# Moving vector work between the units of a fused attention and feed-forward kernel

## The chip, the cores and the metric

The kernel runs on one core of a Trainium2 chip. The metric is the device time of one execution in microseconds (us). Five engines work side by side, each through its own list of instructions in order: TensorE (PE; its weight loads are shown as PEld), VectorE (DVE), ScalarE (ACT), GpSimd (POOL) and SyncE (SP), which only sends transfers. They wait for each other by semaphores.

## What is computed

The input x has 8 sequences of 256 tokens with 256 features. The reference, cut to its core:

```
x = x + attention(layernorm(x), ctx, ctx, mask)   # causal, masked, softmax
y = layernorm(x)
h = silu(y @ w1.T * s1) * (y @ w2.T * s2)         # 256 -> 1024
h = gelu(h @ h1.T * s3)                           # 1024 -> 1024
h = gelu(h @ h2.T * s4)                           # 1024 -> 1024
x = x + h @ w3.T * s5                             # 1024 -> 256
```

All weights are -1, 0 or 1; the scales s1 to s5 are float32.

## The kernel before

**Blocks.** The 2048 tokens are cut into four blocks t = 0 to 3 of 512 tokens, and `pair(s)` (L822) takes two blocks through the feed-forward part: t0 = 2s and t1 = 2s + 1. Everything is held turned, features on the 128 partitions and 512 tokens along a row. One matmul is 128 x 128 weights by 128 x 512 values into one PSUM bank.

**Two parts per value.** TensorE reads a rounded float32 form. Every operand is therefore split: ACT makes the rounded part (oh, `parted`, L786; hyt in `casts`), and DVE the rest (ol, `rest`, L312; lyt in `rests`, L601). Each product runs once with either part.

**Seven products for eight.** The two 1024 x 1024 layers (n = 2 and 3) work on the two blocks together in a scheme of seven products of half size instead of eight. `a`, `b` are the upper and lower halves of block t0's hidden values, `c`, `d` those of t1, each in two pieces `[0]`, `[1]` of 128 x 1024. The scheme needs differences, made by DVE in `sub` (L846): T1 = c - a and T2 = d - T1 among them. Product 6 reads T2, product 5 reads T1.

**Units.** `pair` is a generator; what lies between two `yield` is a unit, 80 in each pair:

| units | work of TensorE |
|---|---|
| 0 to 7 | the gated layer of t0: for each o a product pa (w1), then pb (w2); ACT makes gate = silu(pa), DVE multiplies it with pb (L689) |
| 8 to 15 | layer 2, products 1 and 2 |
| 16 to 23 | the gated layer of t1 (c from units 16 to 19, d from 20 to 23) |
| 24 to 43 | layer 2, products 6, 5, 3, 7, 4, four units each |
| 44 to 63 | layer 3, products 1, 6, 5, 3, 7 |
| 64 to 67 | layer 3, product 2 (`second`, L934; tile p); DVE adds each bank to na (L942, recorded at L844) |
| 68 to 71 | layer 3, product 4 |
| 72 to 75 | last layer of t1 (tile po), `finish` (L696) makes res and stores it |
| 76 to 79 | last layer of t0, in the same way |

Before a product, `before_` (L914) fetches the weights after the next (POOL's queue, tile a) and makes the next operand.

**The plan.** After each unit, the loop at L1183 runs what `at` has put into `plan` for (s, unit), in the order in which it was put there (L1164 to L1182). Three kinds of work go in this way:

- The attention of a later block (`stages`, L454), a generator of which each entry runs one stage. Block 2 is prepared in the first pair, block 3 from unit 55 of the first pair to unit 13 of the second. Late stages: bn_stats and bn_aggr of the sum (`sums`, L257; stf and mvf), the root on ACT (sdf, L638), its reciprocal on DVE (L640), `on_all` (L386), which turns the statistics by TensorE (tmf), copies them by DVE (hmf) and spreads them over all partitions by SP's transfers through memory (mf), then `turned_x` (xst), the difference on DVE and the product on POOL (yf, L648 and L649), the casts (hyt), the rests (lyt) and the store of xst (kept).
- Quarter sums of the weights (`sum_up`, L769).
- Looks (`look_through`, L222): the weights are checked for values for which the two-part scheme would not be exact. A step sends the next piece of weights on SP (tile raw, 512 KB, three buffers) and, from the third step on, examines the piece sent two steps before: pieces of w1, w2 and w3 by a TENSOR_REDUCE on DVE (L212), pieces of h1 and h2 by a Sign on ACT (L216) and, a step later, a count on DVE (L218). Four steps are in the first pair, 21 in the second. At the end the verdict decides whether the whole is done again in plain float32.

**Banks.** PSUM has three pools of two buffers: `ps_mm` (p, po, pb of a pair's first block and pa of its second), `ps_x` (px_u, px_y, pa of the first block, and the first po of t0) and `ps_at` (attention, pb of the second block). A product into a bank waits until the reader of its last content is done: the na for p, L689 for pb, L700 for po, the gate for pa.

Of the kernel before, what the change touches and what calls it, by code (L numbers as in the profile page):

```python
# [74 lines left out]
def _network(ctx, tc, g, exact, flag):  # L75
# [20 lines left out]
    def new(p, shape, tag, name, dt=F32, **kw):  # L96
        return p.tile(shape, dt, tag=tag, name=f"{v}{name}", **kw)

    def groups(t):

        return ((0,), (1,)) if t == 0 else ((0, 1),)
# [54 lines left out]
    def keep_warm(times):  # L156
        if exact:
            return
        warm = ps_mm.tile([P, TB], F32, tag="mm", name="warm")
        for _ in range(times):  # L160
            nc.tensor.matmul(warm, lhsT=zeros[:, :P], rhs=zeros[:, :TB], start=True, stop=True)
# [116 lines left out]
    def normed(src, js, mv, y, name):  # L278
        scaled(src, range(NT)[tiles(js)], mv, turned_over(js, root(js, mv, name), name), y)
# [12 lines left out]
    def turned(y, js, name, pool_=None, tag="at", room=None):  # L292

        wide = len(js) * S
        room = room or TB // wide
        pieces = []
        for c0 in range(0, ND, room):
            pt = (pool_ or ps_at).tile([P, room, wide], F32, tag=tag, name=f"{v}{name}_{c0}")
            for c in range(room):
                for n, i in enumerate(range(NT)[tiles(js)]):  # L300
                    nc.tensor.transpose(  # L301
                        pt[:, c, bass.ts(n, P)], y[:, i, bass.ts(c0 + c, P)], ident
                    )
            pieces.append((slice(c0, c0 + room), pt))
        return pieces
# [6 lines left out]
    def rest(lo, value, hi):  # L312
        nc.vector.tensor_tensor(lo, value, hi.bitcast(F32), ALU.subtract)  # L313
# [22 lines left out]
    def table(t, js, func):  # L336

        if t == 0 and js == groups(t)[0 if func == AF.Exp else -1]:
            nc.scalar.activation(junk, eps, func)

    def near(t):

        return exact or t < 2
# [110 lines left out]
    def stages(t, js, once, result, xs, kt, vs, mi):  # L454
# [99 lines left out]
        if first_:  # L554
# [17 lines left out]
            def shifted(i, engine):  # L572
                engine.tensor_scalar(
                    y[:, i, :],
                    xs[:, i, :],
                    centre[:, i : i + 1],
                    std[:, i : i + 1],
                    ALU.add,
                    ALU.mult,
                )  # L580
# [20 lines left out]
        def rests(values):  # L601
            for c, value in values if not exact else ():
                rest(yt[1][:, c, cols], value, yt[0][:, c, cols])

        def turned_x():
            pxt = turned(xs, js, f"pxt_{t}_{js[0]}")
            if t:
                residual_turned(pxt)
            return pxt

        def residual_turned(pxt):
            for c, pt in pxt:
                nc.scalar.copy(xst[:, c, cols], pt)

        if near(t):
            y = once("y", "yf", [P, NT, D])
            if first_:
                residual_turned(turned_x())
                shifted(1, nc.vector)
            else:  # L620
                normed(xs, js, mvf, y, f"f_{t}_{js[0]}")
            table(t, js, AF.Silu)
            yield
            pxt = None if first_ else turned_x()
            if not t and js == groups(t)[-1]:
                keep_warm(WARM_LATER)
            yield

            where = () if t else (ps_mm, "mm") if first_ else (ps_x, "x", 1)
            values = turned(y, js, f"pyt_{t}_{js[0]}", *where)  # L630
            casts(values)
            if not t and not first_:
                residual_turned(pxt)
            yield
            rests(values)
        else:
            std = once("sq", "sdf", [P, NT], tiny, bufs=2)
            nc.scalar.activation(std, mvf[:, 1, :], AF.Sqrt, bias=eps)  # L638
            yield
            nc.vector.reciprocal(mvf[:, 1, :], std)  # L640
            yield
            mean, rstd = on_all(mvf, ("row", "row2"), f"mf_{t}")
            yield
            turned_x()
            yield
            y = once("y", "yf", [P, ND, TB])
            for c in range(ND):
                nc.vector.tensor_tensor(y[:, c, :], xst[:, c, :], mean, ALU.subtract)  # L648
                nc.gpsimd.tensor_tensor(y[:, c, :], y[:, c, :], rstd, ALU.mult)  # L649
            yield  # L650
            values = [(slice(c, c + 1), y[:, c : c + 1, :]) for c in range(ND)]
            casts(values)
            yield
            rests(values)
        if js == groups(t)[-1]:
            nc.sync.dma_start(out=kept(t), in_=xst)
        result[:] = yt
# [124 lines left out]
    def half(tag, name):  # L782

        return new(hp, [P, 2, TB], tag, name, bufs=2)
# [37 lines left out]
    def pair(s, places, stock):  # L822
# [9 lines left out]
        def two(names):  # L832
            return [[None, None] for _ in names]
# [12 lines left out]
        def sub(out, one, other):  # L846
            nc.vector.tensor_tensor(out, one, other, ALU.subtract)

        a, b, c, d, T1, T2 = two("abcdef")
# [13 lines left out]
        place = dict(zip(("a", "b", "c", "d", "T1", "T2", "free"), places))  # L863
# [33 lines left out]
        for n in (2, 3):  # L897
            first_, name = n == 2, f"{s}_{n}"
# [63 lines left out]
            if first_:  # L962
                for u in range(QK):
                    second(u)
                    yield
                X.pop(2)
                for o in range(NH):
                    mine, key, k = (c, "c", o) if o < QK else (d, "d", o - QK)
                    if k % 2 == 0:
                        mine[k // 2] = half(place[key], f"h{key}_{s}_{k}")  # L970
                    gated(
                        t1,
                        ready[t1],
                        o,
                        mine[k // 2][:, k % 2, :],
                        ps_mm.tile([P, TB], F32, tag="mm", name=f"pa_{t1}_{o}"),
                        ps_at.tile([P, TB], F32, tag="at", name=f"pb_{t1}_{o}"),
                    )
                    if not s and o in (2, 4):
                        fetch(o // 2 + 1)  # L980
                    if o in (2, 4):
                        T1[o // 2 - 1] = half(place["T1"], f"T1_{name}_{o}")
                        sub(T1[o // 2 - 1], c[o // 2 - 1], a[o // 2 - 1])

                    if o == 5:
                        T2[:] = [half(place["T2"], f"T2_{name}_{h}") for h in range(2)]
                        sub(T2[0], d[0], T1[0])
                    if o == 6:
                        X[6] = parted(T2[:1], f"{name}_6")
                        rest(X[6][0][1], T2[0], X[6][0][0])  # L990
                        sub(T2[1][:, 0, :], d[1][:, 0, :], T1[1][:, 0, :])
                    if o == 7:
                        hi, lo = (
                            new(hp, [P, 2, TB], f"op{i}", f"o{i}_{name}_6_1", FR, bufs=4)
                            for i in "hl"
                        )
                        X[6].append((hi, lo))
                        nc.scalar.copy(hi[:, 0, :], T2[1][:, 0, :])
                        sub(T2[1][:, 1, :], d[1][:, 1, :], T1[1][:, 1, :])
                        nc.scalar.copy(hi[:, 1, :], T2[1][:, 1, :])  # L1000
                        for k in range(2):
                            rest(lo[:, k, :], T2[1][:, k, :], hi[:, k, :])
                    yield
# [28 lines left out]
            for u in range(QK):  # L1032
                before_(3, u)
                product(stock[n, 3], X[3], x[u // 2][:, u % 2, :], u, start=False)
                if u % 2:
                    h = u // 2
# [9 lines left out]
            for u in range(QK):  # L1046
# [4 lines left out]
                if u % 2:  # L1051
                    h = u // 2
# [12 lines left out]
            for u in range(QK):  # L1065
# [4 lines left out]
                if u % 2:  # L1070
                    h = u // 2
# [7 lines left out]
            a, b, c, d, T1, T2 = na, nb, nc_, nd, nT1, nT2  # L1079
            place = at_  # L1080
# [53 lines left out]
    looking = look_through()  # L1134
# [6 lines left out]
    def at(s, units, action):  # L1141
        for unit in units if isinstance(units, (tuple, list, range)) else (units,):
            plan.setdefault((s, unit), []).append(action)
# [13 lines left out]
    def sums_from(r):  # L1157
# [5 lines left out]

    stages_at(1, (0, 0), (0, (1, 2, 4, 5, 7, 9, 10, 10, 10, 11, 13, 14)))  # L1164
    stages_at(
        2, (0, 8), (0, (25, 28, 30, 41, 45, 46, 49, 51, 53, 54, 55, 57, 58, 61, 62, 63))
    )
    stages_at(
        3, (0, 30), (0, (55, 56, 59, 70, 73, 74, 75, 77, 78, 79)), (1, (0, 1, 5, 8, 10, 13))
    )  # L1170
    at(0, (7, 7, 14, 15), lambda: next(summing[2], None))
    at(0, 9, lambda: sums_from(0))
# [1 line left out]
    at(0, 21, lambda: sums_from(1))  # L1174
    at(0, (32, 33, 34, 37), lambda: next(summing[4], None))
    at(0, 44, lambda: w3.extend(load_weight(g.w3t, "w3_")))
    at(0, (72, 74, 76, 78), lambda: next(looking, None))
    looks = (1, 3, 5, 8, 10, 12, 14, 16, 17, 19, 26, 27, 42, 44, 46, 47, 50, 51, 54, 55, 58)
    at(1, looks, lambda: next(looking, None))
    at(1, 61, lambda: [None for _ in looking])  # L1180
# [66 lines left out]
```

## Time and profile before

| what | value |
|---|---|
| median of three runs | 347.38 us (347.16 to 348.01) |
| the profiled execution's own time | 347.29 us |
| its span, first to last instruction | 345.4 us |
| busy: PE, DVE, ACT, POOL | 333.6, 270.1, 216.5, 36.5 us |
| chain that ended last | PE 87%, DVE 7%, ACT 2%, all else 4% |
| DMA | 68.81 MB, mean 199 GB/s |
| start of the first pair's units 17 and 24 | 61.04 and 73.87 us |
| start of units 64, 68, 72 of the first pair | 154.23, 162.24, 169.49 us |
| start of the second pair | 189.94 us |

A row of a timeline gives the start in us, the length in us, the engine, the line of the kernel, the operation, the tiles as out<-in, the shape and how many operations are merged; in brackets the idle time before it and what ended it. The view of waits gives who waited for whom, the total in us, how often and the longest.

### The profile page before, as it was taken

The page shows a single profiled execution, that of the slowest core. Times are in us where ns is not written, and L with a number is a line of the kernel's source. Part 1 is how long each engine was busy: PE and PEld are TensorE (multiplying, and loading weights), DVE is VectorE, ACT ScalarE, POOL GpSimd, SP SyncE. Part 2 cuts the span into 40 slices and gives each one's busy share as a digit, 9 for nine tenths or more (in the row PEclk, how much of TensorE's full clock was granted, in tenths as well). Part 3 has the DMA queues.
Part 4 walks back from the last instruction along what each step waited for, and adds up shares of the span by engine and source line. Part 5 has one row for each costly group of instructions (what it writes and reads, how often), then busy time and mean ns, then how long its engine had stood idle before and what let it go on. Part 6 is the DMA issues. An engine that isn't in the chain of part 4 may idle for free.

```text
span 345.4 us, 4324 instructions
## 1 busy us (share of the span) xinstructions
PE 333.6 (97%) x1505; PEld 269.6 (78%) x1506; DVE 270.1 (78%) x411; ACT 216.5 (63%) x300; POOL 36.5 (11%) x78
## 2 busy tenths in 40 slices
PE   8799999999999999999999999999999999999992
PEld 3677888787888888887888788887788888888781
DVE  5679866999799938687887894899957989756761
ACT  4668735358946755757672565556896688767630
POOL 3520000210001410022000003000001000000000
PEclk9999999999999999999999999999999999999998
DMA  5999981899396833369516482970644589630032
GB/s 184 344 297 272 254 297 61 319 316 278 133 361 238 244 123 121 131 240 328 188 74 232 143 258 99 283 283 28 227 139 138 164 260 372 225 121 0 0 122 71
DMA packets 20702, 68.81 MB, mean 199 GB/s; under 512 B 2465, under 2 KB 5313, under 8 KB 17090
## 3 DMA queue, kind: packets, MB, share of 16 engines
q0 software_dynamic: 7488, 36.70, 33.2%
q1 hardware_dynamic: 13040, 31.63, 26.8%
q8 instruction: 14, 0.23, 0.3%
q14 instruction: 14, 0.11, 0.1%
q10 hardware_dynamic: 146, 0.13, 0.1%
HBM read 55.86 MB, written 8.40 MB: 186 GB/s over the span
## 4 chain that ended last, share of the span: by engine, by line
PE 87%; DVE 7%; ACT 2%; issue 1%; DMA 1%; POOL 1%; POOLq 0%; ACTq 0%; DVEq 0%
PE px_u L813 34%; PE px_y L813 15%; PE po L1101 8%; PE p L813 7%; PE pa L673 7%; PE pb L673 6%; PE pv L528 3%; PE ps L467 3%; DVE ol L313 1%; PE pqt L301 1%; DVE sta L261 1%; PE pp L510 1%; PE pxt L301 1%; DMA xs<-x 1%; PE pa L879 1%
## 5 line engine op out<-in xcount | busy, mean ns | idle before, releaser
L813 PE MATMUL px_u<-oh,a 128*128 128x512 f32 x256 | 71.4, 394 | 0.4 <-ACT oh L796 0.4
L813 PE MATMUL px_u<-ol,a 128*128 128x512 f32 x256 | 70.8, 391 | 0.0
L813 PEld LDWEIGHTS px_u<-ol,a 128*128 128x128 f32 x256 | 47.9, 188 | 11.5 <-DVE ol L313 1.5
L813 PEld LDWEIGHTS px_u<-oh,a 128*128 128x128 f32 x256 | 47.6, 188 | 10.7 <-ACT oh L796 0.8
L686 ACT ACTIVATE gate<-pa,sc 128x512 f32<-128x512 f32 x32 | 21.8, 687 | 25.1 <-PE pa L673 22.5
L813 PE MATMUL px_y<-oh,a 128*128 128x512 f32 x128 | 34.5, 391 | 0.0
L813 PE MATMUL px_y<-ol,a 128*128 128x512 f32 x128 | 34.2, 389 | 0.0
L813 PEld LDWEIGHTS px_y<-ol,a 128*128 128x128 f32 x128 | 24.0, 188 | 5.0
L813 PEld LDWEIGHTS px_y<-oh,a 128*128 128x128 f32 x128 | 23.9, 188 | 5.0
L757 POOL DMA_DIRECT2D a<-S x16 | 8.5, 534 | 131.8 <-PE px_u L813 55.0
L216 ACT ACTIVATE sign<-raw 128x1024 bf16<-128x1024 f32 x16 | 16.9, 1055 | 7.0 <-DMA raw<-h2q 2.7
L218 DVE SCALAR_TENSOR_TENSOR sign<-raw,sign 128x1024 bf16<-128x1024 f32 x16 | 19.2, 1218 | 0.5 <-ACT sign L216 0.5
L673 PE MATMUL pa<-hyt,w 128*128 128x512 f32 x60 | 19.1, 399 | 0.2 <-DVE na L844 0.2
L673 PE MATMUL pb<-hyt,w 128*128 128x512 f32 x60 | 18.6, 391 | 0.2 <-DVE res L700 0.2
L673 PE MATMUL pa<-lyt,w 128*128 128x512 f32 x60 | 18.5, 390 | 0.0
L673 PE MATMUL pb<-lyt,w 128*128 128x512 f32 x60 | 18.5, 389 | 0.0
L841 ACT ACTIVATE nd<-nd,sc 128x512 f32<-128x512 f32 x16 | 10.7, 715 | 11.7 <-DVE nd L844 11.7
L813 PE MATMUL p<-oh,a 128*128 128x512 f32 x64 | 17.5, 394 | 0.4 <-DVE na L844 0.4
L313 DVE TENSOR_TENSOR ol<-nT,oh 128x1024 fp32r<-128x1024 f32 x12 | 14.5, 1221 | 3.9 <-ACT oh L796 3.8
L813 PE MATMUL p<-ol,a 128*128 128x512 f32 x64 | 17.1, 389 | 0.0
L844 DVE TENSOR_TENSOR na<-p,na 128x512 f32<-128x512 f32 x16 | 10.9, 688 | 7.9 <-PE p L813 7.9
L841 ACT ACTIVATE nb<-nb,sc 128x512 f32<-128x512 f32 x16 | 10.7, 717 | 10.1 <-DVE nb L844 7.4
(196 smaller groups left out, 649.7 us busy)
## 6 DMA issues: line engine op xcount, KB each, us to landing
a<-S POOLq DMA_DIRECT2D x16, 1024.0 KB, 5.0
a<-h1q POOLq DMA_DIRECT2D x6, 1024.0 KB, 8.1
a<-h2q POOLq DMA_DIRECT2D x6, 1024.0 KB, 5.1
raw<-h1q SPq DMA_DIRECT2D x8, 512.0 KB, 4.2
raw<-h2q SPq DMA_DIRECT2D x8, 512.0 KB, 5.1
vs<-ctx_n SPq DMA_DIRECT2D x4, 512.0 KB, 7.7
q<-h1q POOLq DMA_DIRECT2D x4, 512.0 KB, 20.4
q<-h2q POOLq DMA_DIRECT2D x8, 256.0 KB, 13.9
```

The source lines that it names most:

```text
L216: nc.scalar.activation(sign, raw, AF.Sign)
L218: nc.vector.scalar_tensor_tensor(sign, raw, 1.0, sign, ALU.mult, ALU.not_equal, accum_out=count[:, n : n + 1])
L313: nc.vector.tensor_tensor(lo, value, hi.bitcast(F32), ALU.subtract)
L467: nc.tensor.matmul(ps[:, a:e], lhsT=qt[:, c, bass.ts(2 * j + h, P)], rhs=kt[:, j, c, : e - a], start=(c == 0 and t > 0), stop=(c == ND - 1 ...
L528: nc.tensor.matmul(pv[:, h, :], lhsT=prt[:, j, bass.ds(a + k * P, P)], rhs=vs[:, 2 * j + k, :], start=(k == 0), stop=(k == n - 1),)
L673: nc.tensor.matmul(pm, lhsT=wc[:, bass.ts(o, P)], rhs=x, start=(n == 0), stop=(n == len(steps) - 1),)
L686: nc.scalar.activation(gate, pa, AF.Silu, scale=sc[:, 0, o : o + 1])
L757: nc.gpsimd.dma_start(out=a, in_=src)
L813: nc.tensor.matmul(bank, lhsT=a[:, k, bass.ts(o, P)], rhs=x[k // 2][part][:, k % 2, :], start=start and (part, k) == steps[0], stop=stop a ...
L841: nc.scalar.activation(out, src, AF.Gelu, scale=sc[:, n, o : o + 1])
L844: nc.vector.tensor_tensor(out, one, other, ALU.add)
L1101: nc.tensor.matmul(po, lhsT=w3[j * QK + k][:, bass.ts(o, P)], rhs=xs_[j][k // 2][part][:, k % 2, :], start=(j == 0 and (part, k) == STEPS[0]),
```

## The change

Four things move; no operation is added or taken away (the rests of blocks 2 and 3 stand apart instead of together).

- T1: both halves were made on DVE after the gated products of units 18 and 20. Now the first is made at unit 18, and the second at unit 21, behind the first half of T2.
- The rests: `rests` now yields after each of its two rests. Blocks 0 and 1 still run both at once. Block 2's were both at unit 63 of the first pair and are now at units 68 and 69, and the stage behind them (the store of xst, the handing over of the result) at unit 70. Block 3's were both at unit 13 of the second pair and are at 13 and 14.
- Block 3's `on_all` of the sum's statistics moves from unit 1 to unit 2 of the second pair.
- The four look steps of the first pair move from units 72, 74, 76, 78 to 70, 72, 74, 76.

```diff
         def rests(values):
             for c, value in values if not exact else ():
                 rest(yt[1][:, c, cols], value, yt[0][:, c, cols])
+                yield
...
-            rests(values)
+            list(rests(values))
...
-            rests(values)
+            yield from rests(values)
...
-                    if o in (2, 4):
-                        T1[o // 2 - 1] = half(place["T1"], f"T1_{name}_{o}")
-                        sub(T1[o // 2 - 1], c[o // 2 - 1], a[o // 2 - 1])
-
+
+
+                    if o == 2:
+                        T1[:] = [half(place["T1"], f"T1_{name}_{h}") for h in range(2)]
+                        sub(T1[0], c[0], a[0])
                     if o == 5:
                         T2[:] = [half(place["T2"], f"T2_{name}_{h}") for h in range(2)]
                         sub(T2[0], d[0], T1[0])
+                        sub(T1[1], c[1], a[1])
...
-        2, (0, 8), (0, (25, 28, 30, 41, 45, 46, 49, 51, 53, 54, 55, 57, 58, 61, 62, 63))
+        2, (0, 8), (0, (25, 28, 30, 41, 45, 46, 49, 51, 53, 54, 55, 57, 58, 61, 62, 68, 69, 70))
...
-        3, (0, 30), (0, (55, 56, 59, 70, 73, 74, 75, 77, 78, 79)), (1, (0, 1, 5, 8, 10, 13))
+        3, (0, 30), (0, (55, 56, 59, 70, 73, 74, 75, 77, 78, 79)), (1, (0, 2, 5, 8, 10, 13, 14, 14))
...
-    at(0, (72, 74, 76, 78), lambda: next(looking, None))
+    at(0, (70, 72, 74, 76), lambda: next(looking, None))
```

On the engines' lists this is: on TensorE tmf moves from behind pb of unit 1 to behind pb of unit 2; on DVE the second T1, the two lyt of block 2, one lyt of block 3, two reduces and the copy of tmf (hmf) move; on SP the four raw loads move ahead of the transfers of res and out beside them, and one of w3's ahead of mf; ACT and POOL keep their order.

## The prediction

> **What bounds the kernel now.** The page comes first: it names the full engine and shows whether its clock was held back.
>
> ```profile
> PE 333.6 (97%) x1505; PEld 269.6 (78%) x1506; DVE 270.1 (78%) x411; ACT 216.5 (63%) x300; POOL 36.5 (11%) x78
> PEclk9999999999999999999999999999999999999998
> ```
>
> TensorE is busy for 97% of the span, at full clock (digit 9) in all 40 slices but the last. The change removes none of its work, so it can win only where TensorE stands still. The view of waits, cut to 150 to 250 us and to TensorE, lists those places:
>
> ```profile
> PE p L813 <- DVE na L844: 0.4, 1, 0.4
> PE px_u L813 <- ACT oh L796: 0.4, 1, 0.4
> PE tmf L390 <- DVE mvf L640: 0.2, 1, 0.2
> PE pb L673 <- DVE res L700: 0.2, 1, 0.2
> ```
>
> Four waits, and the four parts of the change point at them. The view counts from the modelled end of a pipelined matmul and so understates. I count from start to start: eight px_u matmuls start at 73.87 us and the next eight at 75.68, so one takes 0.2267 us. The timeline of TensorE:
>
> ```profile
> 156.95 1.07 PE L813 MATMUL p<-ol,a 128*128 128x512 f32 x4
> 158.44 0.50 PE L813 MATMUL p<-oh,a 128*128 128x512 f32 x1 [0.43 <-DVE na L844]
> ...
> 192.21 0.61 PE L673 MATMUL pa<-lyt,w 128*128 128x512 f32 x2
> 193.02 0.73 PE L673 MATMUL pb<-hyt,w 128*128 128x512 f32 x2 [0.20 <-DVE res L700]
> 193.59 0.62 PE L673 MATMUL pb<-lyt,w 128*128 128x512 f32 x2
> 194.46 0.27 PE L390 MATMUL tmf<-ident,mvf 128*8 128x128 f32 x1 [0.25 <-DVE mvf L640]
> ```
>
> Four matmuls from 156.95 are through at 157.86, but the next starts at 158.44: 0.58 lost, and 0.11 more because the first matmul after a wait takes 0.34 instead of 0.23. **0.69** at unit 66. In the same way pb is 0.36 + 0.11 late at 193.02, and tmf 0.41 + 0.11 at 194.46: **0.99** together. Product 6 of the second pair could start at 235.42 and starts at 236.01: 0.59 + 0.11 = **0.70**. All four undone: 2.4 us.
>
> **The sum goes part by part.** DVE is the late engine each time. In its rows an operation starts 0.08 us before the end of the one before, or 0.03 after it where it reads that result.
>
> **Third block's rests (units 63 to 68 and 69).** DVE's rows there:
>
> ```profile
> 155.85 1.94 DVE L313 TENSOR_TENSOR lyt<-yf,hyt 128x512 fp32r<-128x512 f32 x2 [0.20 <-ACT hyt L595]
> 157.71 0.68 DVE L844 TENSOR_TENSOR na<-p,na 128x512 f32<-128x512 f32 x1
> 158.31 1.21 DVE L313 TENSOR_TENSOR ol<-nT,oh 128x1024 fp32r<-128x1024 f32 x1
> 159.44 0.68 DVE L844 TENSOR_TENSOR na<-p,na 128x512 f32<-128x512 f32 x1
> ```
>
> The two lyt rests stand ahead of the first na, which frees the PSUM bank for the third p product. Without them na runs when its product ends (156.21): 156.3 to 157.0, and the wait at 158.44 is gone. What is late next is the second na, behind the ol. The ol reads ACT's oh<-nT, which runs 156.97 to 158.02 and is not moved (it stands behind ACT's casts, these behind POOL's products): ol 158.05 to 159.27, na 159.19 to 159.87. The fourth p product then wants its bank at 157.86 + 1.81 = 159.67 and gets it at 159.92: 0.25 + 0.11 lost again. Gain 0.69 - 0.36 = **0.33**; bounds 0 and 0.69.
>
> The first lyt takes 1.11 of the 1.94 and the second 0.69: POOL's second product runs until 156.41 beside the first. The Trainium skill (SBUF — State Buffer, section SBUF: two separate sides) has a lock for this: a DVE operation with two SBUF inputs and a GpSimd one that reads SBUF exclude each other. By it the moved rests would each be 0.69, and the first na, with one input from PSUM, would not be held; the sum stays as it is, because ACT's oh sets the ol.
>
> In their new place (167.3 us on) the rests delay nb, qt and the ol of the last layer by 1.2 us. TensorE needs those ol only at 176.4 and has them at 174.4. ACT's Exp follows at 178.7 instead of 178.06; the transposes that read it are due at 179.2. Cost nothing, with 0.5 us of cover; beyond that, us for us. The last block's split rests delay one look's count by 0.55 us (219.98 to 220.53), and through its load a later one; that enters the T1 sum below.
>
> **Looks two units sooner, statistics a unit later.** DVE before the end of the first pair:
>
> ```profile
> 191.12 1.19 DVE L212 TENSOR_REDUCE seen<-raw 128x1 f32<-128x1024 uint16 x1
> 192.22 0.74 DVE L700 SCALAR_TENSOR_TENSOR res<-po,s,res 128x512 f32<-128x512 f32 x1
> ```
>
> The reduce leaves this place, so res ends near 191.8, its bank is free before pb wants it (192.66), and 0.47 is won. The reduces now stand at units 74 and 76, one more than before between 179 and 188. DVE's idle time there pays: its rows have gaps of 0.05, 0.27, 0.42 and 0.97 us before the res at 188.32. Followed through, xs ends at 187.2 and that res is due at 188.0: 0.7 us of cover. The raw loads go out earlier on SP (the second beside the first at 157 us instead of 180.55), ahead of the waiting store of res, so they are there.
>
> tmf now follows pb of unit 2 and finds mvf done (194.41): 0.52 won, of which its insertion keeps 0.11, as behind the other transposes of this kind. Next late is ACT: the statistics end at 191.20, Sqrt 0.30, a table load of 1.28 (191.55 to 192.84), then the gate, until 193.54. The third pa reuses the bank that this gate reads and is now due at 189.94 + 16 x 0.2267 = 193.57. That is a tie, since both move together; I charge one restart, 0.11. Gain 0.99 - 0.11 - 0.11 = **0.77**; bounds 0.3 and 0.9.
>
> Against this speaks the Trainium skill (ScalarE: Activation LUTs, section What ACT_TABLE_LOAD costs), which puts a switch of tables at about 2.66 us with its drain. An estimate by that page: the gate 1.38 later and the gain lost. The trace differs (the gate starts 0.01 after the 1.28 us load), and the measurement decides.
>
> The copy of tmf on DVE moves behind an ol, from 195.0 to 197.7. SP's three mf transfers follow, about 2.7 us later (mf landed at 202.1), against a use at 209.75: nothing.
>
> **T1's second half, both pairs.** The second T (1.22 us) moves behind hd of unit 21 and the T that reads it, to shorten the way to oh. In the first pair DVE's rows are:
>
> ```profile
> 68.73 0.75 DVE L689 SCALAR_TENSOR_TENSOR hd<-pb,sc,gate 128x512 f32<-128x512 f32 x1
> 69.40 1.22 DVE L847 TENSOR_TENSOR T<-hc,ha 128x1024 f32<-128x1024 f32 x1
> 70.53 0.75 DVE L689 SCALAR_TENSOR_TENSOR hd<-pb,sc,gate 128x512 f32<-128x512 f32 x1
> 71.31 1.23 DVE L847 TENSOR_TENSOR T<-hd,T 128x1024 f32<-128x1024 f32 x1
> 72.45 0.74 DVE L689 SCALAR_TENSOR_TENSOR hd<-pb,sc,gate 128x512 f32<-128x512 f32 x1
> 73.66 1.23 DVE L313 TENSOR_TENSOR ol<-T,oh 128x1024 fp32r<-128x1024 f32 x1 [0.46 <-ACT oh L796]
> ```
>
> Here the T at 69.40 fills time in which DVE must wait: hd at 70.53 needs pb of unit 21, whose last matmul ends at 70.41. Put behind, it leaves DVE empty from 69.48 to about 70.5 and is paid later. New order: hd 70.52, T2 71.30 to 72.52, T1 72.44 to 73.66, hd 73.58 to 74.33, ol from 74.25: 0.59 later than 73.66; ACT's oh (then 72.56 to 73.61) is not what it waits for. The gap of 0.46 is used up, the empty stretch of 1.05 is new. DVE then runs without a gap to the ol of product 5, which TensorE already waits for (it starts that matmul at 82.85, 0.06 after that ol). TensorE is late by the same: cost **0.59**; bounds 0 and 0.7. No wait follows in which it could be regained.
>
> In the second pair hd of unit 21 came late itself (232.87), and pb was ready at 232.0: there the gap of 0.46 is truly saved. The start of product 6 no longer waits (oh done 235.2, due 235.4). But the later ol of products 6 and 5 set the end (240.59 to a matmul at 240.64), and DVE's gain up to there is 0.46 less the slip of hd of unit 20 (0.37 from the later Sign and gate, less 0.14 no longer waited): **0.23** of the 0.70; bounds 0 and 0.7.
>
> **Sum:** 0.33 + 0.77 + 0.23 - 0.59 = 0.74 us won. The profiled execution took 347.29 (span 345.4 and 1.9 around it); it lies 0.09 under the median of 347.38. 347.29 - 0.74 = 346.55, as a median 346.6. A measurement of this kernel tells about 0.3%, 1.04 us, from no change: the line is at 346.34.
>
> **Rivals.**
>
> 1. As summed: 346.6, chance 0.43 (345.9 to 347.1).
> 2. The first pair does not pay: DVE picks up the missing us before product 5, because its rows from 73.2 to 82.79 hold gaps of 0.46, 0.03 and 0.09 and the bank waits are modelled. For it: product 6 starts there without a wait now. Against it: the last ol and its matmul are 0.06 apart. 0.74 + 0.59 = 1.33: 346.0, faster. Chance 0.32.
> 3. The change does not do what it says: each wait is handed to the next in line, the fourth p product takes all of the 0.69 and the third pa waits for its gate, so 0 + 0.3 + 0.23 - 0.59, nothing, is left: 347.4. For it: both successors stand within 0.3 us. Chance 0.17.
> 4. Slower: the reduce at unit 76 waits for its load. If SP sends the second raw load only behind the store of res (180.55, as now), it lands near 187 (one raw load took 7.0 us, from 182.50 to 189.51, others 4.3). The reduce, due at 184.5, holds xs, the statistics, Sqrt and the gate 2.7 us; 0.7 is covered, the third pa is 2.0 late: 346.6 + 2.0 = 348.6. It decides from 0.7 us of lateness and turns the sum at 1.5. Against it: SP's new order has the load ahead of that store. Chance 0.08.
>
> **How the numbers follow.** Likeliest 346.6. Case 1 alone gives 345.9 to 347.1; cases 2 and 3 and the bounds of the terms widen that to 345.6 to 347.6, and case 4 stays out. Faster by 0.3%: case 2 but for 0.02 and a little of case 1 (0.07), 0.37. Slower: case 4 and 0.01 of case 3, 0.09. Within: 0.54.
>
> **What would show it.** No TensorE wait for the first na, res or mvf; a new one of some 0.3 us at the fourth p product for na. In the first pair an idle DVE of 1 us before hd of unit 21, and products 6 and 5 about 0.59 later against pa of unit 16. In the second, px_u without a wait for oh and a gain of 0.2 instead of 0.7 by product 3. I am wrong if the first pair's product 3 starts as early as before, or if DVE stands at units 74 to 79 for a load.

## The result and the profile after

| | before | after |
|---|---|---|
| median of 22 runs each | 347.36 us (346.79 to 349.37) | 348.51 us (347.50 to 349.81) |
| the profiled execution, its span | 347.29, 345.4 us | 348.88, 347.1 us |

The changed kernel is slower: ratio 1.0023, 95% interval 1.0012 to 1.0034 (0.8 us by the ratio, 1.15 by the medians). The prediction was 346.6 us, a little faster, with a range up to 347.6. The median lies above that range, and the sign was wrong.

The page of the changed kernel shows TensorE nearly as full as before, in a span that is 1.7 us longer:

```profile
PE 334.9 (96%) x1506; PEld 269.3 (78%) x1506; DVE 268.9 (77%) x411; ACT 216.2 (62%) x300; POOL 36.6 (11%) x78
PEclk9999999999999999999999999999999999999998
```

The clock is the same in both (mean 0.996) and no matmul was added (the one more in the count is a warm-up matmul whose record is missing before), so the lost time is waiting. The view of TensorE's waits, 150 to 250 us, where before had four:

```profile
PE pa L674 <- ACT gate L687: 0.9, 1, 0.9
PE px_u L814 <- DVE ol L313: 0.3, 1, 0.3
```

All four waits that the change aimed at are gone. In their place stands one that no step of the prediction had on TensorE: a pa product that waits 0.9 us for a gate of ACT. (The 0.3 for ol belongs to products 6 and 5 of the second pair.)

To see where each us went, I set the two executions beside each other matmul by matmul, and took the start in the changed kernel less the start in the one before, each from its span's start. A step in that difference is time won or lost at that place:

| place | shift before it and after it, us | won (+) or lost (-) | predicted |
|---|---|---|---|
| first pair, products 6 and 5 (73.87 to 78.31) | +0.12, +0.69 | -0.57 | -0.59 |
| na and p, units 66 and 68 (158.4 to 160.6) | +0.69, -0.02, +0.33 | +0.36 | +0.33 |
| res, mvf, tmf (193.0 to 196.7) | +0.33, -0.58, -0.46 | +0.78 | +0.77 |
| second pair, pa of unit 20 (228.17) | -0.46, +0.74 | **-1.20** | -0.37, counted within T1 |
| second pair, products 6 and 5 (236.0 to 240.6) | +0.74, +0.18, +0.76 | -0.02 | +0.60, less that 0.37: +0.23 |
| 291 to 297 us | +0.76, +1.31 | -0.55 | 0 |

(The first 0.12 was there before anything that the change touches, and 0.28 of the 1.59 between the two executions lies outside these steps, most of it behind the last matmul.) Up to 228 us the kernel was 0.46 us ahead. The wait of unit 20 alone turned the sign. TensorE's timeline shows the three places that went as forecast and then the new wait:

```profile
160.62 1.20 PE L814 MATMUL p<-oh,a 128*128 128x512 f32 x4
...
192.99 0.61 PE L674 MATMUL pb<-hyt,w 128*128 128x512 f32 x2
...
193.91 0.73 PE L674 MATMUL pa<-hyt,w 128*128 128x512 f32 x2
...
195.86 0.27 PE L390 MATMUL tmf<-ident,mvf 128*8 128x128 f32 x1
...
227.29 0.61 PE L674 MATMUL pb<-lyt,w 128*128 128x512 f32 x2
...
228.80 0.73 PE L674 MATMUL pa<-hyt,w 128*128 128x512 f32 x2 [0.89 <-ACT gate L687]
```

The pair at 227.29 is through at 227.29 + 2 x 0.2267 = 227.74, and the next starts at 228.80: 1.06 lost, and 0.11 more for the restart (0.73 for two matmuls instead of 0.61), together 1.17; the rest of the table's 1.20 is drift since 197 us. The gate it waits for is on ACT. ACT's timeline, in the kernel before and then in the changed one:

```profile
225.62 1.06 ACT L216 ACTIVATE sign<-raw 128x1024 bf16<-128x1024 f32 x1 [1.03 <-DVE hc L689]
226.58 0.67 ACT L686 ACTIVATE gate<-pa,sc 128x512 f32<-128x512 f32 x1
```

```profile
227.12 1.06 ACT L216 ACTIVATE sign<-raw 128x1024 bf16<-128x1024 f32 x1 [2.95 <-DMA raw<-h1q]
228.08 1.25 ACT L687 ACTIVATE gate<-pa,sc 128x512 f32<-128x512 f32 x2
```

In both, a Sign of the sum's looks stands ahead of the gate in ACT's queue, and the gate starts when the Sign is through. Before, the view puts the Sign's idle time down to DVE's hc, but that had ended at 223.8. The last packets of the raw load landed at 225.54, 0.08 before the Sign: it waited for the load there too. In the changed kernel the load lands at 227.03 and the Sign starts 0.09 later. So the load is **1.49 us** later, although its issue on SP is only 0.18 later. The timeline of all engines at that time, cut to the two issues, in the kernel before and then in the changed one:

```profile
221.23 0.33 SPq L234 DMA_DIRECT2D raw<-h1q  x1
...
221.38 0.53 POOL L757 DMA_DIRECT2D a<-S  x1 [6.67 <-PE p L813]
```

```profile
220.96 0.53 POOL L758 DMA_DIRECT2D a<-S  x1 [6.67 <-PE p L814]
...
221.41 0.33 SPq L234 DMA_DIRECT2D raw<-h1q  x1
```

The **order has turned**. Before, the raw load (512 KB) goes out 0.15 ahead of POOL's weights (1 MB): it takes 4.3 us and the weights 6.7. After, the weights go out 0.45 ahead: they take 5.0 and the raw load 5.6. POOL's issue follows a p product and is earlier by the 0.42 that TensorE had won. SP's issue follows a look's count on DVE, and that is later in spite of the 0.46 won. DVE's rows after:

```profile
217.68 0.68 DVE L313 TENSOR_TENSOR lyt<-yf,hyt 128x512 fp32r<-128x512 f32 x1
218.95 0.69 DVE L845 TENSOR_TENSOR na<-p,na 128x512 f32<-128x512 f32 x1 [0.59 <-PE p L814]
219.56 0.68 DVE L313 TENSOR_TENSOR lyt<-yf,hyt 128x512 fp32r<-128x512 f32 x1
220.16 1.22 DVE L218 SCALAR_TENSOR_TENSOR sign<-raw,sign 128x1024 bf16<-128x1024 f32 x1
```

DVE's rows before:

```profile
218.10 1.28 DVE L313 TENSOR_TENSOR lyt<-yf,hyt 128x512 fp32r<-128x512 f32 x2
...
219.98 1.22 DVE L218 SCALAR_TENSOR_TENSOR sign<-raw,sign 128x1024 bf16<-128x1024 f32 x1
```

Before, both rests of the last block stood ahead of the na, in time in which DVE would otherwise wait for the p product. Apart, the first leaves that time empty (the 0.59), and the second stands between na and the count at 220.16. That count reads the last of a raw buffer, and the next raw load waits for it.

### The profile page after: what moved, and what is told of

Read it like the earlier page. It is cut to its first block, busy times and chain, and to the rows that moved or that the text cites. A ratio compares the mean times of both kernels' runs of the same rounds, so it can differ in the third digit from the quotient of the medians.

```text
span 347.1 us, 4325 instructions
## 1 busy us (share of the span) xinstructions
PE 334.9 (96%) x1506; PEld 269.3 (78%) x1506; DVE 268.9 (77%) x411; ACT 216.2 (62%) x300; POOL 36.6 (11%) x78
## 4 chain that ended last, share of the span: by engine, by line
PE 75%; DVE 11%; DMA 4%; issue 4%; ACT 3%; POOL 1%; DVEq 0%; ACTq 0%; POOLq 0%
PE px_u L814 26%; PE px_y L814 15%; PE po L1104 8%; PE p L814 6%; PE pa L674 4%; PE pb L674 4%; PE pv L528 3%; PE ps L467 3%; DMA raw<-h2q 3%; DVE T L848 2%; DVE ol L313 2%; DMA raw<-h1q 2%; DVE sign L218 1%; DVE hd L690 1%; PE warm L161 1%
```

## The experiments

**Theory A**: the split of the last block's rests is the cause, through this chain: rest, count, raw load behind the weights instead of ahead of them, Sign, gate, PSUM bank, pa. Its rivals (B and C in the expectations) do without the chain and look for the loss in the other parts of the change, T1's new order above all, and in loads that land late by chance. Each kernel was timed beside the kernel before, whose median was 346.85, 346.83 and 347.02 us in the three groups. "Shift" is that of the profiled execution at the end of the kernel, against before, from the comparison matmul by matmul.

**1. The changed kernel, with the last block's rests together again.**

```diff
-        3, ..., (1, (0, 2, 5, 8, 10, 13, 14, 14))
+        3, ..., (1, (0, 2, 5, 8, 10, 13, 13, 13))
```

> The changed kernel with block 3's two rests both at unit 13 of the second pair, as before; all else as changed. Theory A (order of loads): the split put one rest ahead of the look's count of unit 14, the raw load behind that count was sent at 221.41 us, after the 1 MB of weights (220.96) instead of ahead of them (221.23 against 221.38 before), and took 5.6 instead of 4.3 us; the Sign that needs it holds the gates. Then the wait of TensorE for the gate of unit 18 (1.17 us in the changed kernel) is gone here, T1's chain follows on, and the time is 346.6 to 347.1, 1.4 us under the changed kernel's 348.5. Theory B (T1): the new order of T1 costs it in the second pair; the wait stays or turns into one of the same size before product 6, 348.3 to 348.6. Theory C (chance): the loads vary from run to run, and such a wait comes and goes with no regard to the split: 347.4 to 348.5.

Measured: 346.67 us (before 346.85), ratio 0.9993, 0.9979 to 1.0008; shift -0.70. The wait of unit 20 is gone. Raw goes out at 220.75, again 0.15 ahead of the weights, and lands at 225.14. ACT's timeline of this kernel:

```profile
225.22 1.06 ACT L216 ACTIVATE sign<-raw 128x1024 bf16<-128x1024 f32 x1 [1.12 <-DMA raw<-h1q]
226.19 0.67 ACT L687 ACTIVATE gate<-pa,sc 128x512 f32<-128x512 f32 x1
```

One number in the list of places takes the whole loss away. The shift of -0.70 is nearly the 0.74 that the prediction summed.

**2. The kernel before, with that split alone.**

```diff
-        3, ..., (1, (0, 1, 5, 8, 10, 13))
+        3, ..., (1, (0, 1, 5, 8, 10, 13, 14, 14))
```

(`rests` yields as in the change; block 2's two rests stay at unit 63.)

> The kernel before with one edit: block 3's rests at units 13 and 14 instead of both at 13. Theory A: the raw load is sent some 0.4 us behind the weights, lands about 1.5 us later, TensorE waits about 1.1 us for the gate of unit 18, and DVE's chain to products 6 and 5 is late by about 1.5: 348.4 to 349.0. Theory B: nothing happens here, 347.4. Theory C: nothing that the split causes, 347.0 to 347.8.

Measured: 348.91 us (before 346.85), ratio 1.0050, 1.0031 to 1.0069; shift +1.83. From 10 us up to unit 20 the two profiles differ by 0.1 us at most, there +1.09, and +1.65 from product 6 on. TensorE's timeline:

```profile
229.15 0.73 PE L674 MATMUL pa<-hyt,w 128*128 128x512 f32 x2 [0.77 <-ACT gate L687]
```

Here TensorE had won nothing earlier, yet the order turns: weights at 221.43 (4.8 us), raw at 221.88 (5.5 us). The split alone, without T1 and without any other part, costs more than the whole change did. The rivals fall as main causes.

**3. The changed kernel, with the count ahead of the split rest.** The look step of unit 14 is registered before the block's stages, so its count comes first on DVE.

```diff
+    at(1, 14, lambda: next(looking, None))
     stages_at(3, ...)
...
-    looks = (1, 3, 5, 8, 10, 12, 14, 16, 17, ...)
+    looks = (1, 3, 5, 8, 10, 12, 16, 17, ...)
```

> The changed kernel, with the look of unit 14 of the second pair run ahead of block 3's second rest; the rests stay split. Theory A: the raw load goes out ahead of the weights again and the wait for the gate is gone: 346.6 to 347.1, as with the rests together. If the split itself costs the time (the rest delays na and its bank): 348.3 to 348.6. Theory C: 347.4 to 348.5.

Measured: 348.64 us (before 346.85), ratio 1.0048, 1.0031 to 1.0066; shift +1.27. Raw goes out at 220.75 and the gate of unit 18 is in time, but TensorE waits 1.03 two units later, for a gate behind the next Sign. This edit moved something else as well: the store of xst (512 KB) now stands behind that raw load on SP and went out at 221.13 instead of 217.56, into the same 0.4 us as raw and the weights (220.90). The weights took 8.7 us, and the next raw load held its Sign until 231.23. The expectation was missed, for a reason in the experiment.

**4. The same, with the store sent early.** The two edits of number 3 stay, and the store leaves after the first of the two rests, at 217.64 (217.99 in the kernel before).

```diff
-            yield from rests(values)
+            for n, _ in enumerate(rests(values)):
+                if n == 0 and t == 3:
+                    nc.sync.dma_start(out=kept(t), in_=xst)
+                yield
-        if js == groups(t)[-1]:
+        if js == groups(t)[-1] and (exact or t < 3):
```

> As count_first (the changed kernel with the look of unit 14 ahead of block 3's second rest), but with the store of xst sent at unit 13, where it was before; in count_first it had moved behind the raw load and stood beside it and the weights (221.13 us), so that the run told nothing of the split. Theory A (what counts is what is in flight beside the raw loads): loads ahead of the weights and no store beside them: no wait of TensorE for a gate, profile 0.5 to 0.7 us under before, time 346.4 to 346.9 where before is 346.85. If the split itself costs: as the changed kernel, 1.2 us over before, 348.0.

Measured: 346.93 us (before 346.83), ratio 1.0010, 0.9993 to 1.0026; shift +0.06. There is no wait for a gate: raw at 220.90 lands in 4.05 us, ahead of the weights at 221.04. In exchange the second lyt, now behind the count, comes late for pa of unit 16: the shift goes from -0.38 to +0.04 there, 0.4 us lost: the 0.5 to 0.7 under before that was expected of the profile did not come. So the split does not pay even with the load in time. Numbers 3 and 4 differ in the time of one store, and by 1.7 us.

**5. The changed kernel, with the Sign behind the gate.** The split and the late load stay; the look that starts the Sign stands a unit later.

```diff
-    looks = (1, 3, 5, 8, 10, 12, 14, 16, 17, 19, ...)
+    looks = (1, 3, 5, 8, 10, 12, 14, 16, 18, 19, ...)
```

> The changed kernel with the look of unit 17 of the second pair moved to unit 18, so that its Sign stands behind the gate of unit 18 on ACT and not ahead of it. The raw load is as late as in the changed kernel (sent behind the weights, landed near 227.0). Theory A: the late load reaches TensorE only through the Sign in ACT's queue; the wait of 1.17 us for the gate is gone though the load is still late, and the time is 346.6 to 347.2. If the transfers slowed something else (weights, bank): the wait stays, 348.0 to 348.5.

Measured: 346.53 us (before 346.83), ratio 0.9995, 0.9980 to 1.0009; shift -0.48. ACT's timeline:

```profile
225.40 0.69 ACT L687 ACTIVATE gate<-pa,sc 128x512 f32<-128x512 f32 x1 [1.12 <-PE pa L674]
226.98 1.06 ACT L216 ACTIVATE sign<-raw 128x1024 bf16<-128x1024 f32 x1 [0.90 <-DMA raw<-h1q]
```

The load is as late as in the changed kernel (behind the weights by 0.45, 5.4 us, landed 226.90) and the Sign waits for it as there. The gate is ahead of the Sign now, and TensorE does not wait. This shows the last part of the chain: not the late load but the queue behind the Sign is what TensorE paid for.

**6. The kernel before, with the new T1 alone.**

> The kernel before with the new order of T1 alone, both pairs. By the prediction's terms: first pair 0.59 us later from products 6 and 5 on, second pair 0.2 to 0.3 gained by product 5, in all 347.6 to 347.8. Theory B: the whole loss is here, 348.5. If T1 pays in both pairs as meant: 346.6 to 347.0.

Measured: 347.35 us (before 346.85), ratio 1.0013, 1.0000 to 1.0025. The shift is +0.67 behind the first pair's products 6 and 5 and +0.46 behind the second's: 0.6 lost (0.1 of the 0.67 is there before them) and 0.21 won, where the terms expected 0.59 and 0.2 to 0.3. A late load at 290 us adds 0.4, as in the changed kernel.

**7 and 8. The rests together, and T1 new in the second pair only, or old in both.**

```diff
-                    if o == 2:
+                    if not s and o in (2, 4):
+                        T1[o // 2 - 1] = half(place["T1"], f"T1_{name}_{o}")
+                        sub(T1[o // 2 - 1], c[o // 2 - 1], a[o // 2 - 1])
+                    if s and o == 2:
...
-                        sub(T1[1], c[1], a[1])
+                        if s:
+                            sub(T1[1], c[1], a[1])
```

(Number 8 has `if o in (2, 4)` for both pairs, as before.)

> Rests of block 3 together again, and T1's new order in the second pair only; looks, statistics and block 2's rests as changed. The prediction's terms: 0.33 + 0.77 + 0.2 won and nothing lost: profile 1.2 to 1.4 us under before, time 345.6 to 346.2 where before is 346.85. If T1's order costs nothing in the first pair, as the change meant: the same as rests_together, 346.7.

> Rests of block 3 together and T1 as before in both pairs; looks, statistics and block 2's rests as changed. The prediction's terms 0.33 + 0.77: profile 1.0 to 1.2 us under before, time 345.8 to 346.3; 0.2 over t1_second_pair_only, 0.4 under rests_together. If T1 pays in sum: over rests_together, 346.9 to 347.2.

Measured, beside 346.83 before: number 7 346.17 us, ratio 0.9987, 0.9970 to 1.0005, shift -1.11; number 8 346.04 us, ratio 0.9975, 0.9956 to 0.9995, shift -1.38. Against number 1 (346.67, shift -0.70, run beside 346.85) the old T1 in the first pair is worth 0.5 us by the medians and 0.4 by the shifts. In the second pair the new T1 wins nothing: products 6 and 5 give some 0.2 in number 7, and in number 8, with the old order, some 0.35. The 0.13 between the medians is well inside the spread.

**9 and 10. The kernel before, with block 2's rests alone, and with the looks and statistics alone.**

> The kernel before with block 2's rests at units 68 and 69 and its last stage at 70; block 3's both at unit 13. The prediction's term: the wait for the first na gone (0.69), a new one of 0.36 for the second na, 0.33 won: profile 0.25 to 0.45 under before at unit 68, time 346.4 to 346.6 where before is 346.83. If the next na takes all (the prediction's third rival): 346.8. If nothing is late next: 346.1.

> The kernel before with the four looks two units sooner and block 3's statistics turned at unit 2. The prediction's term: 0.99 of waits less 0.11 for the insertion and 0.11 for a restart, 0.77 won: 346.0 to 346.3 where before is 346.83. If the gate's table load holds the third pa (third rival): 0.3 won, 346.5.

Measured, beside 347.02: number 9 346.99 us, ratio 1.0004, 0.9983 to 1.0025. Its shift is +0.19 ahead of unit 66 (from before anything that the edit moves), there -0.51, at unit 68 -0.18, at the end -0.39: 0.70 won and 0.33 paid back. The time alone cannot tell this from nothing; the profile has both steps of the forecast. Number 10: 346.86 us, ratio 0.9976, 0.9957 to 0.9996; the median misses the 346.0 to 346.3 that was expected, the ratio (346.2) does not. Its profiled execution was the slowest of its twelve. By 10 us it was 1.52 late, ahead of anything that the edit moves: its products from 5 to 10 us ran slower (the second to the fifth score product start 0.21 us apart, 0.11 in the kernel before); why is not shown. It then won 0.78 between 193 and 197 us (+1.63 to +0.85).

**11 and 12. The Sign behind the gate, as in number 5, with the rests together; T1 old in both pairs, or new in the second only.**

> t1_old_rests_together with the look of unit 17 moved to unit 18, its Sign behind the gate. Theory A: the gate and with it DVE's hc, T1 and hd no longer hang on when the load lands, so part of the 0.7 before product 6 goes too and fewer executions are slow: profile 1.1 to 1.6 us under before, 345.5 to 346.1. If the Sign of unit 19 sets that chain anyway: as t1_old_rests_together, 346.0.

> t1_second_pair_only with the look of unit 17 moved to unit 18. In the changed kernel this move brought 0.4 us more in front of product 5 than putting the rests together did; so some 0.2 to 0.4 under t1_second_pair_only: 345.6 to 346.0, the lowest of all these kernels. If the Sign of unit 19 sets the chain: as t1_second_pair_only, 346.2.

Measured, beside 347.02: number 11 346.41 us, ratio 0.9986, 0.9970 to 1.0002; number 12 **346.10 us, ratio 0.9972, 0.9956 to 0.9988**, shift -1.15. Number 11 missed what was expected: in its profile the third pa at 193.93 lost 0.6 to a gate that was late because DVE's res had waited for the load of res, and product 6 waited for oh (0.9). Number 12 has the lowest ratio of all and, with number 8, beats both kernels: 0.9 us under before, and by the ratios to before 0.5% under the changed kernel. Between 8 and 12 the intervals tell nothing. The 0.4 that number 12's expectation starts from is not in the traces: in front of product 5, numbers 1 and 5 both gain 0.69, and so do 7 and 12. There, the Sign's place adds nothing once the rests are together.

## Why the prediction was wrong

**Third block's rests: right.** 0.33 forecast, 0.36 measured. The first na no longer holds p, and the second does, for the 0.24 + 0.10 that the shift shows at 160.6 (0.25 + 0.11 in the forecast). The cover behind it held: no wait follows at 176 or 179 us. In number 9 the two steps are 0.70 won and then 0.33 back. In their new place the two rests take 0.69 and 0.68 us, where the first had taken 1.11 beside POOL's product.

**Looks and statistics: right.** 0.77 forecast, 0.78 measured, in the changed kernel and in number 10. pb and tmf start without a wait, the restart of the third pa is there (0.73 at 193.91), and no reduce at units 74 to 79 stands for a load: rival 4's place was wrong.

**T1, first pair: right.** 0.59 forecast, 0.57 measured. DVE's rows in the changed kernel:

```profile
70.64 0.75 DVE L690 SCALAR_TENSOR_TENSOR hd<-pb,sc,gate 128x512 f32<-128x512 f32 x1 [1.03 <-PE pb L674]
71.42 1.23 DVE L848 TENSOR_TENSOR T<-hd,T 128x1024 f32<-128x1024 f32 x1
72.56 1.22 DVE L848 TENSOR_TENSOR T<-hc,ha 128x1024 f32<-128x1024 f32 x1
73.70 0.74 DVE L690 SCALAR_TENSOR_TENSOR hd<-pb,sc,gate 128x512 f32<-128x512 f32 x1
74.36 1.21 DVE L313 TENSOR_TENSOR ol<-T,oh 128x1024 fp32r<-128x1024 f32 x1
```

There is the empty 1.03 ahead of hd, where the T stood, and the ol at 74.36 (74.25 in the forecast, plus the 0.12 of this execution). Rival 2, that DVE would pick this up, fell; number 7 against number 1 gets most of the loss back (0.4 to 0.5) by undoing it.

**T1, second pair, without the slip: too large.** The prediction took 0.46 + 0.14 = 0.60 from the wait for oh, less a slip of 0.37. The term by itself is some 0.2 (numbers 1, 6 and 7). The start of product 6 gains what was forecast, but the last ol of products 6 and 5 come from a DVE without gaps and give most of it back: number 1's shift goes from -0.48 to -1.17 and then to -0.70. The net of 0.23 in the text agrees with that by chance, since it had a slip of 0.37 taken off that these kernels do not have.

**The step that failed** is this one: "The last block's split rests delay one look's count by 0.55 us (219.98 to 220.53), and through its load a later one; that enters the T1 sum below", and there as "0.37 from the later Sign and gate". The chain was named, in its right order; its size was wrong. The text does not say how the 0.37 follows, but it fits the 0.55 less 0.08 (the Sign's start behind its load) and 0.10 (hd of unit 20 behind the count ahead of it, 231.07 against 230.97): a load issued 0.55 later was taken to land 0.55 later, and to reach TensorE only by way of DVE.

Two things were left out. First, the load stood 0.15 ahead of a 1 MB transfer on another queue, so a delay of 0.2 puts it behind: measured 5.4 to 5.6 us in place of 3.9 to 4.4, so 1.49 us for an issue 0.18 later by the clock (0.64 later against TensorE). Second, the gate was not set against the pa that needs its bank. In the kernel before it ended at 227.25, 0.92 ahead of pa of unit 20 (228.17), and TensorE's own lead of 0.46 took half of that. A Sign 0.47 later would about have fitted; it came 1.50 later, because nothing but 0.08 lay between the load and the Sign.

The whole step costs 1.2 us in the changed kernel at unit 20 and takes T1's gain with it; alone it costs 1.65 us in the profile, 2.1 by the median and 1.7 by the ratio (number 2). With 1.20 in place of 0.37, and with no gain of T1's second pair, the prediction's sum is 0.33 + 0.77 - 1.20 - 0.59 = 0.69 us lost: 348.0 for this profile. The other 0.9 of the 348.88 is, within 0.05, the 0.12 at the start, the 0.55 behind 291 us and the 0.28 outside the steps.

No rival had it. Rival 4 was the nearest: a raw load that comes late and an engine standing behind it. It looked at the looks that the change moves by name, and not at the look that only stands behind a moved instruction.

**What stays open.** The sum without the failed step is confirmed by the profile (-0.70 in number 1), but by the median number 1 wins only 0.18, with an interval of -0.7 to +0.3. And the 0.55 lost at 291 to 297 us is not shown to be the change's. ACT's timeline of the changed kernel:

```profile
290.15 1.06 ACT L216 ACTIVATE sign<-raw 128x1024 bf16<-128x1024 f32 x1 [2.48 <-DMA raw<-h2q]
291.12 1.00 ACT L933 COPY nb<-px_u 128x1024 f32<-128x1024 f32 x1
```

A raw load sent at 281.02 landed at 290.07, 9.0 us later, with the weights sent at 281.45 beside it. Before, it took 5.5 (280.25 to 285.76). Number 6 has it too (8.9). In the eleven other kernels the load sent there took 5.6 to 6.8. What decides it stays open.

## What to carry to other kernels

When an instruction is moved in an in-order queue, follow not only the instructions behind it but the transfers that these release, and look at what else is sent within half a us of them: a small delay can turn the order of two loads, and then costs the difference of their landing times, not the delay. An operation that waits for a load should not stand ahead of one that the full engine needs; here one place further back in ACT's queue was worth as much as undoing the split. And a stretch in which an engine waits is the free place for small work: taken from it, the T1 half cost TensorE 0.57, and the rest (0.68 on DVE) put the count behind it 0.64 later against TensorE.

## What the runs showed of the hardware

- **Two loads sent close together are not shared evenly.** A raw load of 512 KB sent 0.15 us ahead of 1 MB of weights landed after 3.9 to 4.4 us (the kernel before and nine of the kernels here) and the weights after 6.3 to 6.8. Sent 0.45 us behind them, raw took 5.4 to 5.6 us (three kernels) and the weights 4.7 to 5.0.
- **A third transfer is dear.** With a 512 KB store 0.2 to 0.4 us behind them, the weights took 8.7 us and the store 8.8; raw, ahead of both, took 5.4 (number 3).
- **The same load, the same place, 5.5 or 9.0 us** (the kernel before and the changed one, at 280 us). The timed runs of one kernel spread by 1 to 3 us, as much as all that this change moves. Whether such loads make that spread is not shown: in number 10's profile 1.5 us of it came in the first 10 us, from slower products.
